# Four graph layers on one core: the order of all jobs of 32 graphs is computed in the kernel's source instead of being interleaved by hand-set start times

## The chip, the core and the metric

The kernel runs on one core of a Trainium2 chip. A core has a tensor engine (PE) that multiplies matrices, and whose weight loads are listed apart as PEld; a vector engine (DVE); an activation engine (ACT); GpSimd (POOL); and a sync engine (SP) that here only issues DMAs. PE reads SBUF and writes PSUM. Each engine works through its own queue in order, and engines wait for each other by semaphores. The metric is the device time of one execution in microseconds; less is better.

## The reference

Thirty-two graphs of 512 nodes with 256 features, each with a symmetric 512 x 512 adjacency, go through four layers. Each layer takes `h = max(layernorm(x), 0)` and adds its result to `x`. In layer 3 the transformer block has its own residuals and norms inside.

```python
def reference(x, adj, ...):                       # x (32, 512, 256) f32, adj (32, 512, 512) int32
    # layer 0: graph attention with 4 heads of 64
    Wh = (h @ W).reshape(B, N, 4, 64)
    e = leaky_relu(e_src[:, :, None] + e_dst[:, None], 0.2)      # e_src, e_dst: Wh times a_src, a_dst
    x = x + elu(softmax(where(adj > 0, e, -1e9), axis=2) @ Wh)
    # layer 1: one head, softmax over the other axis
    hw = h @ W;  e = leaky_relu(s1[:, :, None] + s2[:, None], 0.2)
    x = x + elu(softmax(where(adj > 0, e, -9e15), axis=1) @ hw)
    # layer 2: scores (h * a_0) h^T where adj == 1 (adj is 0 or 1 here)
    x = x + softmax(where(adj == 1, leaky_relu((h * a_0) @ h.T, 0.2), -9e15)) @ h
    # layer 3: transformer block, 8 heads of 32, feed-forward of 1024
    attn = softmax(where(allowed, q @ k.T / sqrt(32), -inf)) @ v
    t = layernorm(h + attn @ Wo.T + bo) * g1 + b1
    u = layernorm(t + relu(t @ W1.T + c1) @ W2.T + c2) * g2 + b2
    x = x + u
```

All data are 32-bit floats; the masks are bf16. One fp32 product of the source is two MATMUL instructions in the trace.

## The kernel before

Everything of interest is in `quick_path`. (`general_path` is a fallback behind a test at the end and does not run on these inputs.) A graph's 512 nodes are four tiles of 128 partitions, numbered by `i` or `j`; the features are two halves, numbered by `k`.

The Python loops unroll the whole program, so all 32 graphs lie in one straight stream of instructions. A graph passes three stages. Stage 0 loads `adj` and `x`, makes the masks (`masks`, L219 to L232: DVE makes a bf16 mask `m`, PE transposes it at L226, DVE copies it to `mT` and makes `m3` for layer 3) and does layer 0. Stage 1 does layers 1 and 2. Stage 2 does layer 3, the transformer block.

A norm (`norm_stats`, `normed`) is a chain: DVE statistics (L164, L165), POOL adds epsilon and takes the power -0.5 (L167, L168), DVE makes the shift (L170), ACT scales four tiles (L176). PE transposes follow (L185 for layers 0 to 2, L197 for layer 3).

Layer 0 computes `wh` (L257), sends per-row factors through DRAM to have them on all partitions (`spread`, L204 to L210), and for each of four heads lets DVE form four tiles `p` (L274) and PE sixteen products (L281). Layer 1 is alike with one head (L308, L320, L321, output products L333). Layer 2 has score products (L358), two exponentials on ACT, two DVE steps, and output products (L370).

Layer 3: products for q and k (L391) and v (L400); then eight steps of two groups of heads by four tiles, each with four score products (L419), two exponentials on ACT of 1024 columns (L430), a mask product on DVE of 2048 columns (L431), four products with v into `ps_ct` (L434) and four with ones into `ps_to` for the sums (L440). The sums of a group go out to DRAM, back in another layout, are inverted, and go out and back again, four DMAs on SP's queue (L448 to L456), and DVE multiplies them in (L459). Then the output projection (L467), an add (L469), a norm with PE transposes (L197) and ACT (L474), the two feed-forward products (L486 with ACT L487, and L493 with DVE L495), a last norm, two POOL operations (L498, L499) and the store (L500).

PSUM: `ps_a` has two tiles of one bank for layers 0 to 2, `ps_b` two tiles of two banks for layer 3, and `ps_ct` and `ps_to` have one bank each. In SBUF most activations of a stage have one buffer, so each stage holds one graph at a time. `x`, `mT` and `m3` have three.

What sets the order: each stage is a generator that yields a share of a period after each piece of work, and the main loop always advances the generator with the least due time. A graph's three stages start 0, 1.3 and 2.38 periods after its number:

```python
    STARTS = (0.0, 1.3, 2.38)
    live = [[b + at, stage(b)] for b in range(B) for at, stage in zip(STARTS, (stage0, stage1, stage2))]
    while live:
        now = min(live, key=lambda one: one[0])
```

That fixes the order in which instructions are written down. The tile framework's scheduler then takes this order as priority, reorders by its own estimates of durations, chooses buffers, and adds all semaphore waits. The scores of layer 3 have raised priority, with one added wait so that four heads go at a time. The final order in each engine's queue is fixed at compile time.

Of the kernel before, what the change touches and what calls it, by code (L numbers as in the profile page):

```python
# [1 line left out]

# [50 lines left out]

def quick_path(
# [21 lines left out]
    work = ctx.enter_context(tc.tile_pool(name="work", bufs=4))  # L76
    small = ctx.enter_context(tc.tile_pool(name="small", bufs=3))
    dram = ctx.enter_context(tc.tile_pool(name="dram", bufs=2, space=bass.MemoryType.DRAM))


    ps_a = ctx.enter_context(tc.tile_pool(name="ps_a", bufs=2, space=bass.MemoryType.PSUM))
    ps_b = ctx.enter_context(tc.tile_pool(name="ps_b", bufs=2, space=bass.MemoryType.PSUM))
    ps_c = ctx.enter_context(tc.tile_pool(name="ps_c", bufs=1, space=bass.MemoryType.PSUM))

    def load(b):
        adj_t = act.tile([P, NT, N], I32, tag="adj", name=f"adj_{b}")
        nc.sync.dma_start(adj_t, adj[b].rearrange("(t p) j -> p t j", p=P))
        x_t = act.tile([P, NT, D], F32, tag="x", name=f"x_{b}", bufs=3)
        nc.sync.dma_start(x_t, x[b].rearrange("(t p) d -> p t d", p=P))
        return adj_t, x_t  # L90

    loaded = {0: load(0)}
# [17 lines left out]
    src_r = rows_of(nc, work, a0_src, D, "src_r", "p", 6)  # L110
    dst_r = rows_of(nc, work, a0_dst, D, "dst_r", "p", 6)
    a1_r = rows_of(nc, work, a1, 2 * D, "a1_r", "p", 6)
# [13 lines left out]
    ff2b_r = rows_of(nc, work, ff2_b, D, "ff2b_r", "p", 6)  # L126
# [4 lines left out]
    for k in range(KD):  # L131
        for a_r, at, sign in ((src_r, D, -1.0), (dst_r, D + H0, 1.0)):
            wa = work.tile([P, N], F32, tag="y", name="wa")
            nc.vector.scalar_tensor_tensor(wa[:, :D], w0_t[:, k, :D], sign, a_r, OP.mult, OP.mult)
            nc.vector.tensor_reduce(
                w0_t[:, k, at : at + H0], wa[:, :D].rearrange("p (h f) -> p h f", h=H0), AX.X, OP.add
            )
        for at, sign in ((0, 1.0), (1, -1.0)):
            wa = work.tile([P, N], F32, tag="y", name="wa")
            nc.vector.scalar_tensor_tensor(  # L140
                wa[:, :D], w1_t[:, k, :D], sign, a1_r[:, at * D : (at + 1) * D], OP.mult, OP.mult
            )
            nc.vector.tensor_reduce(w1_t[:, k, D + at : D + at + 1], wa[:, :D], AX.X, OP.add)
# [3 lines left out]
    bv_w = work.tile([P, N], F32, tag="y", name="bv_w")  # L147
    ps = ps_a.tile([P, N], F32, tag="mm", name="ps_bv")
# [9 lines left out]

    def norm_stats(t):

        st = small.tile([P, NT, 6], F32, tag="st", name="st")
        mv = small.tile([P, NT, 2], F32, tag="mv", name="mv")
        for i in range(NT):
            nc.vector.bn_stats(st[:, i], t[:, i])  # L164
            nc.vector.bn_aggr(mv[:, i], st[:, i])  # L165
        rstd = small.tile([P, NT], F32, tag="rstd", name="rstd")
        nc.gpsimd.tensor_scalar_add(rstd, mv[:, :, 1], EPS)  # L167
        nc.gpsimd.tensor_tensor(rstd, rstd, nhalf, OP.pow)  # L168
        shift = small.tile([P, NT], F32, tag="shift", name="shift")
        nc.vector.scalar_tensor_tensor(shift, mv[:, :, 0], -1.0, rstd, OP.mult, OP.mult)  # L170
        return rstd, shift

    def normed(t, to, func):
        rstd, shift = norm_stats(t)
        for i in range(NT):
            nc.scalar.activation(to[:, i, :D], t[:, i], func, bias=shift[:, i : i + 1], scale=rstd[:, i : i + 1])  # L176
        return to

    def transposed_a(h, tag, name):

        hT = act.tile([P, KD, N], F32, tag=tag, name=name)
        for k in range(KD):
            ps = ps_a.tile([P, NT, P], F32, tag="mm", name="ps_t")
            for i in range(NT):
                nc.tensor.transpose(ps[:, i], h[:, i, ts(k, P)], ident)  # L185
            if k % 2:
                nc.scalar.copy(hT[:, k], ps.rearrange("p a b -> p (a b)"))
            else:
                nc.vector.tensor_copy(hT[:, k], ps.rearrange("p a b -> p (a b)"))
        return hT  # L190

    def transpose_b(t):

        ps = ps_b.tile([P, KD, N], F32, tag="mm", name="ps_t3")
        for k in range(KD):
            for i in range(NT):
                nc.tensor.transpose(ps[:, k, ts(i, P)], t[:, i, ts(k, P)], ident)  # L197
        return ps

    def spread(cols, n, name):  # L200


        ps = ps_a.tile([P, N], F32, tag="mm", name="ps_sp")
        nc.tensor.transpose(ps[: n * NT, :P], cols, ident)  # L204
        r = small.tile([H0 * NT, P], F32, tag="spread", name="spr")
        nc.vector.tensor_copy(r[: n * NT], ps[: n * NT, :P])
        d = dram.tile([n * NT, P], F32, tag=name + "d", name=name + "_d")
        nc.sync.dma_start(d, r[: n * NT])
        t = act.tile([P, n, N], F32, tag=name, name=name)
        nc.sync.dma_start(  # L210
            t, bass.AP(tensor=d.tensor, offset=d.offset, ap=[[0, P], [N, n], [1, N]])
        )
        return t

    def masks(b, adj_t):


        m = act.tile([P, NT, N], BF, tag="e_0", name=f"m_{b}")
        nc.vector.tensor_scalar_max(m, adj_t, 0)  # L219
        kinds = small.tile([P, 1], F32, tag="kinds", name="kinds")  # L220
        nc.scalar.activation(adj_t, adj_t, AF.Relu, bias=none, accum_out=kinds)
        mT = act.tile([P, NT, N], BF, tag="mT", name=f"mT_{b}", bufs=3)
        for j in range(NT):
            ps = ps_a.tile([P, NT, P], BF, tag="mm", name="ps_m")
            for i in range(NT):
                nc.tensor.transpose(ps[:, i], m[:, i, ts(j, P)], ident_b)  # L226
            nc.vector.tensor_copy(mT[:, j], ps.rearrange("p a b -> p (a b)"))
        m3 = act.tile([P, NT, N], BF, tag="m3", name=f"m3_{b}", bufs=3)
        nc.vector.tensor_max(m3, m, mT)
        for i in range(NT):  # L230
            nc.vector.tensor_max(m3[:, i, ts(i, P)], m3[:, i, ts(i, P)], ident_b)
        nc.vector.scalar_tensor_tensor(ok[:, 0:1], kinds, 0.0, ok[:, 0:1], OP.is_le, OP.mult)  # L232
        return mT, m3

    def within(t, n):

        nc.vector.scalar_tensor_tensor(ok[:, :n], t, RANGE, ok[:, :n], OP.is_le, OP.mult)
        nc.vector.scalar_tensor_tensor(ok[:, :n], t, 1.0 / RANGE, ok[:, :n], OP.is_ge, OP.mult)

    S0, S1, S2 = 1 / 24, 1 / 31, 1 / 74
# [4 lines left out]
    def layer0(b, x_t, mT):  # L247
        h = normed(x_t, act.tile([P, NT, D + 1], F32, tag="h_0", name=f"h0_{b}"), AF.Relu)
        hT = transposed_a(h, "hT_0", f"h0T_{b}")
        yield 1 * S0  # L250
        wh = act.tile([P, NT, H0, F0 + 1], F32, tag="wh_0", name=f"wh0_{b}")

        rt = small.tile([P, 3 * H0, NT], F32, tag="rt", name="rt0")
        for i in range(NT):
            ps = ps_a.tile([P, N], F32, tag="mm", name="ps_wh")
            for k in range(KD):
                nc.tensor.matmul(ps[:, : D + 2 * H0], hT[:, k, ts(i, P)], w0_t[:, k], start=k == 0, stop=k == KD - 1)  # L257
            nc.scalar.activation(wh[:, i, :, F0], ps[:, D + H0 : D + 2 * H0], AF.Exp, scale=SLOPE)
            nc.scalar.activation(rt[:, : 2 * H0, i], ps[:, D : D + 2 * H0], AF.Exp, scale=1.0 - SLOPE)  # L259
            nc.vector.tensor_mul(  # L260
                wh[:, i, :, :F0],
                ps[:, :D].rearrange("p (h f) -> p h f", h=H0),
                wh[:, i, :, F0 : F0 + 1].to_broadcast([P, H0, F0]),
            )
            yield 1 * S0
        rows = spread(rt[:, :H0].rearrange("p h t -> p (h t)"), H0, "rows0")
        yield 1 * S0
        o = act.tile([P, NT, D], F32, tag="h_0", name=f"o0_{b}")
        inv = rt[:, 2 * H0 :]
        for hd in range(H0):  # L270
            ps_t = []
            for j in range(NT):
                p = work.tile([P, N], F32, tag="p", name="p0", bufs=6)
                nc.vector.scalar_tensor_tensor(  # L274
                    p, rows[:, hd], rt[:, H0 + hd, j : j + 1], mT[:, j], OP.max, OP.mult
                )
                ps_t.append(p)
            ps = ps_a.tile([P, NT, F0 + 1], F32, tag="mm", name="ps_o")
            for i in range(NT):
                for j in range(NT):  # L280
                    nc.tensor.matmul(  # L281
                        ps[:, i], ps_t[j][:, ts(i, P)], wh[:, j, hd], start=j == 0, stop=j == NT - 1
                    )
                yield 1 * S0
            nc.vector.reciprocal(inv[:, hd], ps[:, :, F0])
            nc.vector.tensor_mul(
                o[:, :, ts(hd, F0)], ps[:, :, :F0], inv[:, hd].unsqueeze(2).to_broadcast([P, NT, F0])
            )

        e = act.tile([P, NT, D], F32, tag="e_0", name=f"e0_{b}")  # L290
        nc.scalar.activation(e, o, AF.Exp)
        nc.vector.scalar_tensor_tensor(e, e, 1.0, x_t, OP.min, OP.add)
        nc.vector.scalar_tensor_tensor(x_t, o, 0.0, e, OP.max, OP.add)
# [729 lines left out]
```

## Time and profile before

| | |
|---|---|
| median of 3 runs | 5052.46 us (5049.55 to 5053.34) |
| the profiled execution | 5052.43 us, its span 5050.7 us |
| instructions | 51957 |
| PE, ACT, POOL busy | 4361.3 us (86%), 1890.0 us (37%), 718.0 us (14%) |
| DVE busy | 2474.6 us (49%) |
| granted PE clock, mean | 0.915 of full speed |
| DMA | 144.58 MB, 29 GB/s on average |

The span runs from the first to the last instruction. Matmuls are pipelined and their ends are modelled, so a busy PE is not a PE at its peak; start-to-start distances say more. "Idle before <-releaser" is the time for which an engine stood still just before an instruction, with what released it. The granted clock is the share of full speed that the throttle allowed to PE.

### The profile page before, as it was taken

To read this page: it belongs to the slowest core of one execution; us is meant where nothing else is said; L and a number is where in the kernel's file an instruction comes from. 1 tells how busy PE (TensorE), PEld (TensorE's weight loads), DVE (VectorE), ACT (ScalarE), POOL (GpSimd) and SP (SyncE) were. 2 spreads that over 40 slices of the span, in tenths; PEclk is the share of its full clock that TensorE was granted. 3 is DMA by queue.
4 is the path that set the end of the run, shared out by engine and by line. 5 is a ranking of instruction groups with operands and counts; after the bars stand their busy time and mean duration, and the time that the engine had idled before them with its cause. 6 is when DMAs were issued, how large, how long until landed. Compare 5 with 4: busy or idle time off the path is not lost. (4 is left out here: it accounts for less than half of the span.)

```text
span 5050.7 us, 51957 instructions
## 1 busy us (share of the span) xinstructions
PE 4361.3 (86%) x20294; PEld 2595.8 (51%) x20294; DVE 2474.6 (49%) x5115; ACT 1890.0 (37%) x3297; POOL 718.0 (14%) x618
## 2 busy tenths in 40 slices
PE   5888889888899888898888898888988888988886
PEld 4555455555455554455554555544555545555543
DVE  4544554444554454544455544445544455544432
ACT  1333433333433333433334333334333343433332
POOL 0011111110111111111101111101111011111111
PEclk7889899989999999999899999999999989999998
DMA  2010010010000000100100100001000001000000
GB/s 98 26 34 26 26 34 24 28 34 25 27 26 30 30 26 26 35 24 28 34 26 26 34 24 28 30 22 34 25 27 34 26 26 34 24 28 22 5 13 14
DMA packets 95435, 144.58 MB, mean 29 GB/s; under 512 B 25168, under 2 KB 61520, under 8 KB 91088
## 3 DMA queue, kind: packets, MB, share of 16 engines
q1 hardware_dynamic: 88832, 136.21, 8.1%
q10 hardware_dynamic: 6352, 4.99, 0.3%
q8 instruction: 162, 2.65, 0.2%
q14 instruction: 89, 0.73, 0.1%
HBM read 122.96 MB, written 18.22 MB: 28 GB/s over the span
## 5 line engine op out<-in xcount | busy, mean ns | idle before, releaser
L431 DVE TENSOR_TENSOR p<-p,m 128x2048 f32<-128x2048 f32 x256 | 586.0, 2289 | 391.9 <-ACT p L430 384.5
L281 PEld LDWEIGHTS ps_o<-wh,p 128*128 128x128 f32 x4096 | 586.4, 212 | 240.3 <-issue 129.9
L430 ACT ACTIVATE p<-ps_s 128x1024 f32<-128x1024 f32 x512 | 501.6, 1019 | 455.6 <-PE ps_to L440 326.3
L281 PE MATMUL ps_o<-wh,p 128*128 128x65 f32 x4096 | 606.7, 294 | 67.3 <-DVE p L274 66.9
L486 PE MATMUL ps_f<-tT,ff_t 128*128 128x512 f32 x1024 | 582.2, 706 | 73.9 <-ACT f L487 46.6
L274 DVE SCALAR_TENSOR_TENSOR p<-rows,rt,mT 128x512 f32<-128x512 f32 x512 | 458.9, 918 | 98.6 <-PE ps_o L281 82.7
L493 PE MATMUL ps_f<-ff_t,f 128*128 128x256 f32 x2048 | 458.4, 380 | 2.0 <-DVE u L495 2.0
L176 ACT ACTIVATE h<-x,shift,rstd 128x256 f32<-128x256 f32 x512 | 268.9, 591 | 484.2 <-DVE shift L170 197.8
L167 POOL TENSOR_SCALAR rstd<-mv 128x4 f32<-128x4 f32 x192 | 55.6, 294 | 2701.1 <-DVE mv L165 2701.1
L440 PE MATMUL ps_to<-p,ones 128*32 128x512 f32 x2048 | 428.7, 606 | 0.0
L493 PEld LDWEIGHTS ps_f<-ff_t,f 128*128 128x128 f32 x2048 | 387.0, 190 | 73.5 <-issue 15.3
L486 PEld LDWEIGHTS ps_f<-tT,ff_t 128*128 128x128 f32 x1024 | 212.7, 222 | 345.2 <-issue 171.4
L419 PE MATMUL ps_s<-qk 32*128 32x512 f32 x2048 | 350.3, 643 | 30.3 <-ACT qk L392 24.9
L434 PE MATMUL ps_ct<-p,v 128*32 128x512 f32 x2048 | 346.5, 610 | 14.5 <-DVE p L431 14.5
L487 ACT ACTIVATE f<-ps_f,ff1b_c 128x512 f32<-128x512 f32 x256 | 175.3, 685 | 384.6 <-PE ps_f L486 384.6
L333 PE MATMUL ps_o<-wh,p 128*128 128x256 f32 x1024 | 269.1, 402 | 15.5 <-ACT wh L325 15.5
L358 PE MATMUL ps_e<-h2T,ha 128*128 128x512 f32 x512 | 254.0, 621 | 24.7 <-DVE ha L352 23.8
L333 PEld LDWEIGHTS ps_o<-wh,p 128*128 128x128 f32 x1024 | 187.2, 195 | 129.9 <-issue 60.0
L391 PE MATMUL ps_qk<-h3T,wqkv_t 128*128 128x512 f32 x512 | 245.8, 616 | 3.1 <-ACT h3T L381 3.1
L370 PE MATMUL ps_o<-h,p 128*128 128x257 f32 x1024 | 245.5, 382 | 1.5 <-DVE p L364 0.5
L370 PEld LDWEIGHTS ps_o<-h,p 128*128 128x128 f32 x1024 | 192.3, 191 | 53.1 <-issue 24.3
L260 DVE TENSOR_TENSOR wh<-ps_wh,wh 128x256 f32<-128x256 f32 x128 | 54.3, 424 | 317.1 <-ACT rt L259 317.0
(125 smaller groups left out, 5384.8 us busy)
## 6 DMA issues: line engine op xcount, KB each, us to landing
adj<-in_adj_dram SPq DMA_DIRECT2D x32, 1024.0 KB
rows<-rows_d SPq DMA_DIRECT2D x32, 1024.0 KB
x<-in_x_dram SPq DMA_DIRECT2D x32, 512.0 KB
rows<-rows_d SPq DMA_DIRECT2D x32, 512.0 KB
inv<-in_d SPq DMA_DIRECT2D x64, 256.0 KB
out_dram<-y SPq DMA_DIRECT2D x32, 512.0 KB
ff_t<-in_L_gnn_W_dram ACTq DMA_DIRECT2D x2, 1024.0 KB
to_d<-to SPq DMA_DIRECT2D x64, 8.0 KB
```

Source lines behind the costliest of these rows:

```text
L176: nc.scalar.activation(to[:, i, :D], t[:, i], func, bias=shift[:, i : i + 1], scale=rstd[:, i : i + 1])
L274: nc.vector.scalar_tensor_tensor(p, rows[:, hd], rt[:, H0 + hd, j : j + 1], mT[:, j], OP.max, OP.mult)
L281: nc.tensor.matmul(ps[:, i], ps_t[j][:, ts(i, P)], wh[:, j, hd], start=j == 0, stop=j == NT - 1)
L333: nc.tensor.matmul(ps[:, i], p[:, j, ts(2 * g + i, P)], wh[:, j, :D], start=j == 0, stop=j == NT - 1)
L370: nc.tensor.matmul(ps[:, : D + 1], p[:, j, ts(i, P)], h[:, j], start=j == 0, stop=j == NT - 1)
L419: mm = nc.tensor.matmul(ps[r // 2][:, r % 2], qk[at, KD + g, ts(j, P)], qk[at, g], start=True, stop=True)
L430: read = nc.scalar.activation(p[:, 2 * q : 2 * q + 2], ps[q], AF.Exp)
L431: nc.vector.tensor_mul(p, p, m3[:, j : j + 1].to_broadcast([P, HG, N]))
L434: nc.tensor.matmul(ps_ct[at], v[:, j, g * P + r * HD : g * P + (r + 1) * HD], p[:, r], start=j == 0, stop=j == NT - 1,)
L440: nc.tensor.matmul(ps_to[at], ones, p[:, r], start=j == 0, stop=j == NT - 1)
L486: nc.tensor.matmul(ps[:, q], ff1_t[:, k, ts(f, P)], tT[:, k], start=k == 0, stop=k == KD - 1)
L493: nc.tensor.matmul(ps[:, i], f1[f][:, f % 4, ts(i, P)], ff2_t[:, f], start=f == 0, stop=f == NF - 1)
```

## The change

A planner (`Plan`) takes the place of the generators. Instead of emitting an instruction, each step of each layer puts down a job: its engine, how long it occupies the engine (`takes`), when its result is there (`ends`), and what it reads and writes. Durations are constants written into the source: for DVE 0.155 us and 1.04 ns a column, for ACT 0.2 us and 0.81 ns, for a product of 512 columns 0.862 us (`FULL`), of 256 columns 0.432 us, for a step of four score heads 1.2 us, and so on. Buffers are `Kind`s with a number of slots; most are given out in the order in which the tiles were made (`in_turn`).

After the jobs of all 32 graphs are put down, graph by graph, `order` walks through time. At each moment each engine that is free takes, among the jobs whose inputs and slots are there, the one with the least key (graph number, then number of the job). `carry_out` then emits the jobs by planned start, with the planned slot, and ties each instruction to the one before it on its engine by an edge that only orders. Where a slot passes to a tile whose first engine is another one, a wait is added. PE's jobs are single products or short groups, and jobs of different graphs may alternate between them.

Beside this: within the layers the order of a few steps differs (the statistics of all four tiles come before their aggregates; the transposes of layer 3 go tile by tile; the tests `within` of layer 3 come after the add). The second feed-forward product goes into two tiles of `ps_a` where it went into one of `ps_b`. `ha` has the shape of `wh1`. The setup borrows other buffers. The counts and shapes of the products, DVE and ACT operations and DMAs stay as they are.

```diff
+class Plan:
+    HOP = 0.06
...
+    def put(self, engine, takes, ends, outs, ins, call, port=False):
+        j = Job()
+        j.key, j.engine, j.takes, j.ends, j.call, j.port = (self.key, len(self.jobs)), engine, takes, ends, call, port
...
+    def order(self):
+        engines = ("PE", "DVE", "ACT", "POOL", "SP")
...
+                while waiting[e]:
+                    key, one = heapq.heappop(waiting[e])
+                    take, then = slots(one)
+                    if take is not None:
+                        j = one
+                        break
...
+                j.start = max(now, port) if j.port else now
+                free[e] = j.start + j.takes
...
+                end = j.start + j.ends + self.HOP
...
+        return sorted(begun, key=lambda j: j.start)
+
+    def carry_out(self):
...
+        for j in self.order():
...
+                h.tile = kind.pool.tile(
+                    h.shape, h.dtype, tag=f"{kind.tag}_{h.slot}", name=h.name, bufs=1
+                )
...
+            for i in made:
+                if j.engine in last:
+                    self.tc.add_manual_dep(i, last[j.engine].name, edge, reason="as planned")
+                last[j.engine] = i
+            for kind, s in firsts:
+                if kind.last[s] is not None and kind.last[s][0] != j.engine:
+                    self.tc.add_manual_dep(made[0], kind.last[s][1].name, wait, reason="in turn")
...
+    def pool(self, method, *args, fixed=0.1, each=2.2e-3, **kw):
+        return self._do("POOL", self.nc.gpsimd, method, fixed, each, width(args), args, kw, True, 0.03)
...
+    K = {
+        tag: Kind(act, tag, slots)
+        for tag, slots in dict(
+            adj=1, x=3, mT=3, m3=3, h0=1, h0T=1, wh0=1, rows0=1, e0=1, p=6,
+            h1=1, h1T=1, wh1=1, rows1=1, p1=1, y=4, x2=2,
+            h3=1, hT3=1, qk=1, vt=1, p3=2, to=2, inv3=2, n=1,
+            kinds=2, rt0=2, rt1=2, inv2=2, part=4,
+        ).items()
+    }
...
+    K |= {"ps_ct": Kind(psum, "ps_ct", 1), "ps_to": Kind(psum, "ps_to", 1)}
+    K |= {"ps_a": Kind(psum, "ps_a", 2, False), "ps_b": Kind(psum, "ps_b", 2, False)}
...
-                p = work.tile([P, N], F32, tag="p", name="p0", bufs=6)
-                nc.vector.scalar_tensor_tensor(
-                    p, rows[:, hd], rt[:, H0 + hd, j : j + 1], mT[:, j], OP.max, OP.mult
+                p = new("p", "p0", [P, N])
+                plan.dve(
+                    "scalar_tensor_tensor", p, rows[:, hd], rt[:, H0 + hd, j : j + 1], mT[:, j], OP.max, OP.mult
                 )
...
+        for g in range(NT // 2):
+            ps = new("ps_a", "ps_f2", [P, 2, D])
...
-    STARTS = (0.0, 1.3, 2.38)
-    live = [[b + at, stage(b)] for b in range(B) for at, stage in zip(STARTS, (stage0, stage1, stage2))]
-    while live:
-        now = min(live, key=lambda one: one[0])
...
+    for b in range(B):
+        plan.key = b
+        adj_t = new("adj", f"adj_{b}", [P, NT, N], I32)
+        plan.dma(adj_t, adj[b].rearrange("(t p) j -> p t j", p=P), 9.0)
+        x_t = new("x", f"x_{b}", [P, NT, D])
+        plan.dma(x_t, x[b].rearrange("(t p) d -> p t d", p=P), 6.0)
         mT, m3 = masks(b, adj_t)
...
+        layer0(b, x_t, mT)
+        x_t = layer1(b, x_t, mT)
+        layer2(b, x_t, mT)
+        layer3(b, x_t, m3)
+    plan.carry_out()
```

## The prediction

> **What bounds the kernel now.** I read the page first, then the busy time by stretches, then the order of work on the tensor engine (PE), and last the rows of single instructions. The page says PE, and also that PE is not full: 86% busy, at a clock row that dips below 9 here and there.
>
> ```profile
> PE 4361.3 (86%) x20294; PEld 2595.8 (51%) x20294; DVE 2474.6 (49%) x5115; ACT 1890.0 (37%) x3297; POOL 718.0 (14%) x618
> ```
>
> The kernel does 32 equal graphs, so one period is what counts. Line L469 runs once per graph, and its first and last start give the period: (4995.1 - 288.0) / 31 = 151.84 us, with 288.0 before the first and 55.6 after the last.
>
> ```profile
> L469 DVE TENSOR_TENSOR t<-ps_wo,h x32: 1224/1225/1226, 288.0 to 4995.1; 128x1024 f32<-128x1024 f32 x32
> ```
>
> The busy time by stretches, for one period cut at four places (columns: stretch, length, busy us of PE, weight loads, DVE, ACT, POOL, granted clock, DMA share, GB/s):
>
> ```profile
> 2000.88:2032.66 31.78, 31.78 (x131) 24.00 (x129) 7.67 (x28) 6.98 (x18) 0.00 (x0) 1.00 0.10 34
> 2032.66:2047.78 15.12, 11.77 (x85) 10.46 (x84) 12.96 (x20) 7.23 (x17) 7.77 (x6) 1.00 0.01 2
> 2047.78:2115.61 67.83, 64.22 (x354) 30.63 (x354) 38.63 (x57) 31.64 (x48) 6.50 (x6) 1.00 0.10 28
> 2115.61:2150.60 34.99, 23.50 (x73) 12.30 (x73) 18.74 (x56) 13.11 (x20) 8.36 (x8) 0.80 0.12 39
> ```
>
> The feed-forward stretch is full. The last one is not: PE sits idle for 11.5 of 35 us and the clock falls to 0.80. Its order of work shows why:
>
> ```profile
> 2115.61 3.65 PE L358 MATMUL ps_e<-h2T,ha 128*128 128x512 f32 x8
> 2123.62 0.69 PE L226 MATMUL ps_m<-ident_b,m 128*128 128x128 bf16 x5 [4.36 <-DVE m L219]
> 2124.22 4.69 PE L467 MATMUL ps_wo<-wo_t,cT 128*128 128x256 f32 x14
> 2128.75 0.55 PE L226 MATMUL ps_m<-ident_b,m 128*128 128x128 bf16 x7
> 2130.56 0.38 PE L226 MATMUL ps_m<-ident_b,m 128*128 128x128 bf16 x4 [1.26 <-DVE mT L227]
> 2134.75 2.80 PE L197 MATMUL ps_t<-ident,n 128*128 128x128 f32 x8 [3.81 <-ACT n L176]
> ```
>
> PE's queue is in order. Its head is the next graph's mask transposes, which wait 4.36 us for DVE; then come transposes that wait 3.81 us for a norm. Meanwhile the middle graph's last p of layer 2 is written at about 2124.8, and its 7 us of output products (L370) run only from 2150.60. So this is a wait of order, not of data. It recurs in almost every graph:
>
> ```profile
> PE ps_m L226 <- DVE m L219: 132.2, 30, 5.6
> PE ps_t L197 <- ACT n L176: 122.3, 35, 5.4
> ```
>
> **The full-speed content of a period.** Matmul records overlap, so I take start to start where the clock is 1.00. For example 8 of L370 take 1.74 us and 4 of L486 take 1.72:
>
> ```profile
> 2000.88 1.91 PE L370 MATMUL ps_o<-h,p 128*128 128x257 f32 x8
> 2002.62 1.88 PE L486 MATMUL ps_f<-tT,ff_t 128*128 128x512 f32 x4
> 2004.34 1.05 PE L257 MATMUL ps_wh<-w_t,h0T 128*128 128x264 f32 x4
> ```
>
> Per graph, instructions times spacing: layer 3 (qk 16, 7.0; v 16, 3.9; scores 64, 8.6; ct 64, 7.0; to 64, 7.8; wo 16, 3.5; 16 transposes, 1.8; ff1 32, 13.8; ff2 64, 13.8) 67.2 us. The rest (L281 128, 15.5; L257 and L308 3.7 each; L333 7.3; L358 7.3; L370 7.0; 42 mask, norm and spread transposes, 4.3) 48.8 us. Together 116 us. Of 151.84 us, then, 36 are lost. In the period shown idle takes 18.4 of them (149.72 - 131.27), the slow clock some 6.5 (the last stretch holds about 17 us of content in its 23.50 busy), and the rest hides in the modelled busy time.
>
> **The change, part by part.** (1) The arithmetic stays: same matmuls, same DVE and ACT operations, same DMAs. Regrouping of tiles and the reordered statistics cost nothing, since the counts and shapes are the same. (2) The hand-set starts (0, 1.3, 2.38) and yields go, and with them the scheduler's own choice. A greedy plan takes their place: at each free engine the ready job of the oldest graph, then that of the next. The edges inside an engine are order only. The added cross-engine waits fire when a slot passes to a tile with another first engine; the slot was already awaited for its readers, so they add at most queue events (21 ns each in L274's rows) on perhaps ten tiles, 0.2 us a graph. Below nothing they cannot go; I take 0. (3) ff2 leaves the two large PSUM tiles for the two small ones. That frees ps_b for the next graph's layer 3 some 14 us earlier, and ties one of the small tiles for 6.9 us twice, while PE is full of ff2 anyway. I take 0, with ends of -3 (the next h3 transposes start earlier) and +2 (two 0.9 us ps_o jobs must drain first). (4) DMAs keep the SP queue, now in planned order. A transfer that waits for its source holds back those behind it, adj and x loads among them, but these are fetched a graph ahead. I take 0.
>
> What is left is how dense PE becomes. With the oldest graph first, layer 3 runs nearly alone at its own pace. Its chain: norm, transposes and copy 7 (statistics 1.0, POOL 0.23 + 1.04, shift 0.16, four ACT 2.08, transposes 0.3, copy 1.01, hand-overs); qk and v 10.9; attention 34 (eight loops of scores 1.07, two exps of 1.02 and hand-overs, 3.5 each, and 6 for the last product); the round trip of the sums 9.2 (2111.76 to the last issue at 2118.50 in this trace, and some 2.5 to land); cT 0.7, wo 3.5, t 1.2; norm to tT 7; ff1 13.8; ff2 with its add 14.5. That is 102 us with 67 of its own PE work, so 35 us of gaps. The younger graphs have 48.8 us of PE work to put there.
>
> How well are gaps filled? The attention stretch above packs about 57 us of content into 67.83 (84%), the poor one 17 into 35 (49%). Two younger chains of DVE, ACT and DMA steps feed the gaps, so I take three quarters: 26 us. The other 22.6 us come after layer 3, in the rest of the next graph's layers 1 and 2, at 80%: 28. So 102 + 28 = 130, and 1 us for filler jobs that cannot be interrupted: 131 us a graph. The best I can argue is 90% and 95% (102 + 18 = 120), the poorest half and 70% (102 + 45 = 147).
>
> The ends: graph 0 is held by its due times now (its layer 0 ends at about 79, h1T is copied at 101.3; its first product with the sums is at 261.7 and t only at 288.0). As the oldest it runs unhindered, so I take off 12, 7 and 24: t at 245, with 235 and 260 as bounds. The tail stays at 55, one graph alone.
>
> Sum: 245 + 31 x 131 + 55 = 4361, and the 1.7 us that the profiled execution (5052.43) has beside its span (5050.7): 4363. That execution stands 0.03 us from the median. I say 4360.
>
> **One rule against the plan.** DVE and POOL can block each other:
>
> ```profile
> 2041.87 0.72 DVE L274 SCALAR_TENSOR_TENSOR p<-rows,rt,mT 128x512 f32<-128x512 f32 x1
> 2042.73 2.36 POOL L498 TENSOR_TENSOR y<-y,g_r 128x1024 f32<-128x1024 f32 x1 [1.74 <-ACT y L176]
> 2042.84 5.57 DVE L274 SCALAR_TENSOR_TENSOR p<-rows,rt,mT 128x512 f32<-128x512 f32 x2
> ```
>
> Two L274 took 5.57 us beside POOL's large operations, against 0.74 each. Their mean is 918 ns against a median of 743, so 16 x 0.175 = 2.8 us a graph. The plan counts 0.687 for each and never sets its port flag for DVE. I keep 2.8 us of DVE time, inside the 80%. The Trainium skill (SBUF — State Buffer, Who interferes with whom) says more: any DVE instruction with two SBUF inputs and a GpSimd instruction that reads SBUF exclude each other for the whole instruction. By it 49 us of DVE work per graph are exposed to 14.4 us of POOL work, an estimate of 14.4 x 49 / 131 = 5.4 us a graph, and the total would be some 80 us higher than mine; no row of this trace shows the other DVE lines blocked.
>
> **The rivals.** *Starved middle graph (slower).* Oldest first gives the middle graph's layers 1 and 2 only leftovers. Unhindered they take about 60 us (two norms with transposes 12, products 3.7 + 7.3 + 7.3 + 7.0, spread 8, DVE and ACT steps 15). If all of it is left when layer 3 ends, the period is 102 + 60 = 162 and the total 245 + 31 x 162 + 57 = 5324. It decides from the point where more than 50 of the 60 us are left (102 + 50 = 152). Against it: 35 us of gaps, of which these layers need 28. Chance 0.12, slower cases short of full starvation included. *Drift.* The queues are in order, and fillers are placed the moment that the plan thinks them ready. Where DVE is late (L274, and up to 2.87 us once), PE's head waits, and the clock falls again as at 2124. Half of the gain is lost: period 143, total 245 + 31 x 143 + 57 = 4735. Chance 0.22. *Nearly packed.* Attention is planned at 3.4 us a step where rows give 2.93, so real PE runs ahead and the slack absorbs lateness; the clock stays at 1.00. Period 121, total 4053. Chance 0.16. *Nothing happens*, because the order in the queues comes out as before: 0.02; the explicit edges speak against it.
>
> **How the numbers follow.** My forecast has 0.48. The range takes in the nearly packed case with its lower bound (235 + 31 x 120 + 57 = 4012) and drift up to the poorest period (260 + 31 x 147 + 57 = 4874), and leaves out starvation and a little below. A run differs from no change from 0.2% on, about 10 us. Faster: 0.48 + 0.22 + 0.16, less 0.01 for the part of drift that goes too far, 0.85; same 0.02; slower 0.13.
>
> **What would show it.** Right: L469 every 131 us, L226's and L197's PE waits gone as heads of long idles, the clock at 0.96 or more, L370 of the next graph inside layer 3's norm. Wrong: idle PE before scores or before L308 to L370 just after an ff2 (starvation), PE waits on L274 or on DMA rows all over (drift), a clock still at 0.92.

## The result and the profile after

The change made the kernel slower: a median of 5321.59 us (5308.6 to 5335.09) against 5051.01 us (5037.19 to 5053.34) for the kernel before on the same chip, a ratio of 1.054 (95% interval 1.051 to 1.058). That is outside the predicted range. The total lies 2 us from the starved rival's 5324, and the period on it; the experiments show that this is an accident.

The profiled execution took 5324.7 us, its span 5322.9, with a mean granted clock of 0.888 (0.915 before). The first line is the busy time of each engine, the second the once-per-graph add that was L469. (In this kernel one helper line, L292, carries all DVE, ACT and POOL work, L310 the DMAs, and L320 and L322 PE's transposes and products; one reads by tiles.)

```profile
PE 4288.2 (81%) x20294; PEld 2583.6 (49%) x20294; DVE 2622.7 (49%) x5115; ACT 1896.6 (36%) x3297; POOL 751.4 (14%) x618
L292 DVE TENSOR_TENSOR t<-ps_wo,h x32: 1224/1225/1225, 237.8 to 5265.2; 128x1024 f32<-128x1024 f32 x32
```

PE is busy 73 us less than before in a span 272 us longer. The period is (5265.2 - 237.8) / 31 = 162.2 us where it was 151.84. The ends did shorten: the first add comes at 237.8 instead of 288.0. All of the loss lies in the steady state.

What PE waited for (total us, times, longest):

```profile
PE ps_ct L322 <- DVE p L292: 204.3, 140, 5.0
PE ps_wo L322 <- DVE cT L292: 149.0, 32, 10.7
PE ps_t L320 <- ACT n L292: 132.2, 32, 6.8
PE ps_f L322 <- ACT f L292: 100.5, 128, 0.8
```

The mask transposes, the largest wait before, are gone from the top. The norm's transposes kept theirs (122.3 before). Three waits are new or grown. Before, they stood at:

```profile
PE ps_ct L434 <- DVE p L431: 14.5, 34, 1.4
PE ps_wo L467 <- DVE cT L459: 26.7, 17, 6.9
PE ps_f L486 <- ACT f L487: 46.6, 29, 2.4
```

PE waited there for the masked `p` of layer 3, for `cT` and for ACT's `f`. Now the last comes 128 times, four in every graph, always about 0.8 us. A wait that recurs so exactly is built in.

DVE's own waits tell where its delay comes from; both of these stand in its list in every trip of the sums, two in each graph:

```profile
DVE cT L292 <- DMA inv<-in_d: 266.9, 64, 5.9
DVE part L292 <- DMA part<-to_d: 144.5, 64, 8.5
```

One such trip, from the order of work (start, duration, engine, work, and in brackets the idle time before it with its releaser):

```profile
2508.53 0.50 SPq L310 DMA_DIRECT2D to_d<-to  x1
2510.25 0.32 SPq L310 DMA_DIRECT2D part<-to_d  x1
2511.86 0.25 DVE L292 RECIPROCAL part<-part 128x16 f32<-128x16 f32 x1 [5.49 <-DMA part<-to_d]
2512.14 0.33 SPq L310 DMA_DIRECT2D in_d<-part  x1
2513.59 0.55 SPq L310 DMA_DIRECT2D inv<-in_d  x1
2518.69 0.69 DVE L292 TENSOR_TENSOR cT<-cT,inv 128x512 f32<-128x512 f32 x1 [4.19 <-DMA inv<-in_d]
2519.44 4.54 PE L322 MATMUL ps_wo<-wo_t,cT 128*128 128x256 f32 x12 [3.64 <-DVE cT L292]
```

From the first issue to the multiply are 10.16 us. DVE stands 5.49 and 4.19 us at the heads that the plan put there, and PE stands 3.64 us at its own. The granted clock pays too (stretches of 4 us, columns as in the prediction):

```profile
2516.00:2520.00 4.00, 0.56 (x3) 0.51 (x4) 1.31 (x4) 0.44 (x1) 0.00 (x0) 1.00 0.13 49
2520.00:2524.00 4.00, 4.00 (x12) 3.23 (x11) 2.37 (x8) 0.00 (x0) 0.10 (x1) 0.57 0.39 117
```

PE does 0.56 us of work in the first stretch, and in the next the clock is at 0.57.

**The plan against the chip.** The kernel's source ends its planning with a span of its own (`self.span`, no measurement): 4454.9 us for this kernel, with adds from 193.5 to 4404.3, a period of 135.8. Set job by job beside the trace, the chip is 44 us behind the plan at the first add and 861 us at the last, and the lag grows nearly in a straight line (by 21 to 30 us from graph to graph): 26.4 us a graph (162.2 - 135.8). So the plan is about as dense as forecast (135.8 against 131); the chip doesn't follow it. Two places in the source explain much of this.

*The DMAs.* In `order` a job that needs another job of its own engine becomes ready when that one's `takes` is over. For DVE or PE that is right. For SP `takes` is the issue, 0.1 us, not the landing. So the plan lets `part<-to_d` start 0.10 us after `to_d<-to`, and `inv<-in_d` 0.10 us after `in_d<-part`. In the trace the medians from issue to issue are 1.72 and 1.44 us. The plan also lets `inv` arrive 2.8 us after its issue, where the trace has 5.05 to the multiply. A trip planned at 5.4 to 6.1 us takes 10.3 (median of 64, 9.7 to 12.7).

*The halves of a two-bank tile.* Each tile of the first feed-forward takes four products, two for each bank, and ACT reads each bank by itself. The plan counts banks of 512 columns apart, so it has PE fill the second while ACT reads the first. The tile framework tracks the tile as a whole: its wait holds the fourth product until ACT has read the first half.

```profile
2536.93 3.70 PE L322 MATMUL ps_f<-tT,ff_t 128*128 128x512 f32 x8 [0.84 <-ACT f L292]
2541.41 3.70 PE L322 MATMUL ps_f<-tT,ff_t 128*128 128x512 f32 x8 [0.78 <-ACT f L292]
2545.89 2.41 PE L322 MATMUL ps_f<-tT,ff_t 128*128 128x512 f32 x5 [0.78 <-ACT f L292]
```

After every eight instructions, the four products of one tile, PE stands for 0.8 us. Against the plan a feed-forward loses 4.5 us here, and the products for q and k, built alike, 2.1 (medians of the 32 graphs).

### The profile page after: what moved, and what is told of

Same layout as the page of the kernel before. It is cut to its first block, busy times and chain, and to the rows that moved or that the text cites. A ratio compares the mean times of both kernels' runs of the same rounds, so it can differ in the third digit from the quotient of the medians.

```text
span 5322.9 us, 52024 instructions
## 1 busy us (share of the span) xinstructions
PE 4288.2 (81%) x20294; PEld 2583.6 (49%) x20294; DVE 2622.7 (49%) x5115; ACT 1896.6 (36%) x3297; POOL 751.4 (14%) x618
## 5 line engine op out<-in xcount | busy, mean ns | idle before, releaser
L322 PE MATMUL ps_o<-wh,p 128*128 128x65 f32 (+1 forms) x5120 | 826.2, 323 | 83.4 <-DVE o L292 63.7
L322 PEld LDWEIGHTS ps_o<-wh,p 128*128 128x128 f32 x5120 | 779.1, 217 | 178.2 <-issue 100.7
L292 DVE TENSOR_TENSOR p<-p,m 128x2048 f32<-128x2048 f32 x256 | 584.4, 2288 | 221.8 <-ACT p L292 221.7
L292 ACT ACTIVATE p<-ps_s 128x1024 f32<-128x1024 f32 x512 | 495.6, 1020 | 255.2 <-PE ps_s L322 255.2
L322 PE MATMUL ps_f<-tT,ff_t 128*128 128x512 f32 x1024 | 496.3, 623 | 101.4 <-ACT f L292 100.5
L292 POOL TENSOR_SCALAR rstd<-mv 128x4 f32<-128x4 f32 x192 | 74.9, 390 | 3249.0 <-DVE mv L292 2473.4
L322 PE MATMUL ps_ct<-p,v 128*32 128x512 f32 x2048 | 306.4, 673 | 205.0 <-DVE p L292 204.3
L322 PE MATMUL ps_f<-ff_t,f 128*128 128x256 f32 x2048 | 451.3, 380 | 9.1 <-DVE h2T L292 9.1
L292 DVE SCALAR_TENSOR_TENSOR p<-rows,rt,mT 128x512 f32<-128x512 f32 x512 | 403.1, 842 | 92.5 <-DMA rows<-rows_d 92.5
L292 ACT ACTIVATE h<-x,shift,rstd 128x256 f32<-128x256 f32 x512 | 270.1, 592 | 454.3 <-DVE shift L292 368.4
L322 PEld LDWEIGHTS ps_f<-ff_t,f 128*128 128x128 f32 x2048 | 387.7, 190 | 71.8 <-DVE h2T L292 12.8
L322 PEld LDWEIGHTS ps_f<-tT,ff_t 128*128 128x128 f32 x1024 | 191.2, 198 | 392.5 <-ACT f L292 207.0
L322 PE MATMUL ps_e<-h2T,ha 128*128 128x512 f32 x512 | 301.5, 731 | 62.0 <-DVE o L292 48.7
L292 ACT ACTIVATE y<-ps_e,nshift 128x512 f32<-128x512 f32 x256 | 161.2, 681 | 516.1 <-PE ps_e L322 516.1
L322 PE MATMUL ps_s<-qk 32*128 32x512 f32 x2048 | 300.7, 657 | 50.9 <-ACT p L292 49.8
L292 ACT ACTIVATE f<-ps_f,ff1b_c 128x512 f32<-128x512 f32 x256 | 175.9, 687 | 438.5 <-PE ps_f L322 436.8
L292 DVE TENSOR_TENSOR u<-ps_f,n 128x512 f32<-128x512 f32 x64 | 44.3, 692 | 569.2 <-PE ps_f L322 569.2
L322 PE MATMUL ps_wo<-wo_t,cT 128*128 128x256 f32 x512 | 190.2, 537 | 149.0 <-DVE cT L292 149.0
L320 PE MATMUL ps_t<-ident,h 128*128 128x128 f32 x1024 | 251.8, 361 | 69.4 <-ACT h L292 61.1
L322 PE MATMUL ps_to<-p,ones 128*32 128x512 f32 x2048 | 303.0, 666 | 0.0
L322 PE MATMUL ps_qk<-h3T,wqkv_t 128*128 128x512 f32 x512 | 253.7, 634 | 43.1 <-ACT qk L292 38.1
L320 PEld LDWEIGHTS ps_t<-ident,h 128*128 128x128 f32 x1024 | 145.9, 180 | 232.6 <-ACT h L292 130.2
```

What stands on the lines that cost most here:

```text
L292: return [getattr(unit, method)(*map(real, args), **{k: real(v) for k, v in kw.items()})]
L320: made.append(self.nc.tensor.transpose(*map(real, c)))
L322: made.append(self.nc.tensor.matmul(*map(real, c[:3]), start=c[3], stop=c[4]))
```

## The experiments

Theory A: the chip drifts behind because the plan's DMA times are too short. Theory B: it drifts because of the two-bank tiles. Rival C: the starved middle graph. The kernels are `after` with the edits shown. Each row has the plan's own span, the measured median, the ratio to the kernel before with its interval, and the granted clock.

| kernel | edits | own plan, us | chip, us | ratio (95%) | clock |
|---|---|---|---|---|---|
| after | | 4455 | 5321.59 | 1.054 (1.051 to 1.058) | 0.888 |
| e9_sums | two DMA edits | 4431 | 4958.17 | 0.984 (0.981 to 0.986) | 0.923 |
| e1_dma | three DMA edits | 4319 | 4802.77 | 0.952 (0.951 to 0.954) | 0.947 |
| e2_bank | tiles as a whole | 4446 | 5113.44 | 1.015 (1.013 to 1.017) | 0.896 |
| e3_both | e1 and e2 | 4328 | 4619.76 | 0.917 (0.914 to 0.920) | 0.950 |
| e4_noedge | no order edges | 4455 | 5255.9 | (one run) | 0.879 |
| e5_middle | middle graph first | 4447 | 5286.55 | 1.049 (1.046 to 1.051) | 0.888 |
| e6_ctpool | multiply on POOL | 4451 | 5263.2 | 1.045 (1.042 to 1.047) | 0.897 |
| e7_portdur | e3, times, port | 4474 | 4730.66 | 0.939 (0.937 to 0.941) | 0.927 |
| e8_keys | e7, other priority | 4293 | 4440.07 | 0.881 (0.878 to 0.884) | 0.951 |
| e10_noport | e8 without port | 4188 | 4469.17 | 0.886 (0.883 to 0.890) | 0.954 |
| e11_slack | e8, slack | 4307 | 4420.4 | 0.877 (0.875 to 0.879) | 0.954 |

The kernels ran in several sessions, each with the kernel before beside them; its median there lay between 5041.74 and 5051.01 us, so the differences between medians below are good to some 10 us.

### Longer DMA times in the plan: e1_dma

```diff
-                    k.ready = max(k.ready, free[e] if k.engine == e else end)
+                    k.ready = max(k.ready, free[e] if k.engine == e != "SP" else end)
...
-... [1, N]])), 3.5 + 1.2 * n
+... [1, N]])), 3.2 + 0.5 * n
...
-... [[N, HG], [0, HD], [1, N]])), 2.8
+... [[N, HG], [0, HD], [1, N]])), 5.0
```

No instruction is added or taken away. Only the order changes, by times as the trace shows them. (The second edit shortens the broadcast of `rows`. For layer 0 the plan had it at 8.4 us to DVE; the trace of after has 4.73, the median of the 18 times that DVE waited for it.)

> The plan alone is changed: a DMA that reads what the DMA before it wrote is ready when that one has landed (the plan took the moment of its issue, 0.1 us), inv lands after 5.0 us (was 2.8), and the rows after 3.2 + 0.5 n. The plan's own span goes from 4455 to 4319 us. Theory A (the plan believes in a round trip of the sums of 5.5 us that takes 10.8 on the chip, so DVE's queue stands at the multiply with inv and PE behind it): some 10 of the 27 us a graph by which the chip falls behind the plan go, and the kernel takes about 4319 + 870 - 320 - slow clock = 4750 us (4650 to 4900). Theory B (the two halves of a two-bank PSUM tile serialise, which the plan does not know): little of the lag goes, 5050 to 5200. Theory C (oldest graph first starves the younger graphs): no gain over the changed kernel beyond the plan's own, 5180 or more.

Measured 4802.77 us, 519 less than after, as A expected. DVE's waits:

```profile
DVE part L292 <- DMA part<-to_d: 81.9, 17, 5.8
DVE cT L292 <- DMA inv<-in_d: 17.8, 21, 5.9
```

The wait on `inv` fell from 266.9 to 17.8: the plan now puts other work ahead of the multiply. The clock rose from 0.888 to 0.947 with nothing done to it. The times for `rows` and the sums are told apart by e9_sums below.

### Two-bank tiles as the framework has them: e2_bank

```diff
-    i0, i1 = i0 // 512 * 512, i1 // 512 * 512 + 511
+    i0, i1 = i0 // 1024 * 1024, i1 // 1024 * 1024 + 1023
...
                 for k in range(KD):
                     plan.matmuls(FULL, (ps[:, q], ff1_t[:, k, cut(f, P)], tT[:, k], k == 0, k == KD - 1))
+            for q in (0, 1):
+                f = 2 * g + q
                 plan.act(
```

The four products of a tile come first, then ACT's two reads; the same in the products for q and k.

> Only the two-bank tiles of ff1 and q, k are treated otherwise: all four products first, then the two ACT reads, and the plan counts a two-bank tile as one. The plan's span stays (4446). Theory A: PE's waits of 0.8 to 1.0 us in ff1 and qk go (some 6 us a graph), the stand at inv stays: 5100 to 5200 us. Theory B: most of the lag goes, under 4900. Theory C: no change, 5300.

Measured 5113.44 us, 208 less than after. The lag had given 4.5 + 2.1 = 6.6 us a graph, 211 us in 32 graphs. The time lies in the range given under A. That the tiles make most of the lag, as B had it (under 4900), is refuted; they are a second and smaller cause beside A. What the runs show is a wait that the framework sets; whether the hardware would mind the two engines in the two banks was not tried.

### Both: e3_both

> Both edits together; the plan's span is 4328. If A and B are two separate parts of one cause, both gains add up: 4328 + 870 - 320 - 200 = 4680 and less where the clock stays up, 4450 to 4750 us, faster than the kernel before. Theory C: slower than the kernel before.

Measured 4619.76 us, 702 less than after; the two gains alone make 519 + 208 = 727. They add up nearly, so these are two separate losses. The feed-forward's 32 instructions now run in one piece, and the add's rows give a period of (4561.6 - 240.3) / 31 = 139.4 us:

```profile
2489.56 14.00 PE L322 MATMUL ps_f<-tT,ff_t 128*128 128x512 f32 x32
```

```profile
L292 DVE TENSOR_TENSOR t<-ps_wo,h x32: 1193/1224/1225, 240.3 to 4561.6; 128x1024 f32<-128x1024 f32 x32
```

This kernel's plan has 131.6. So of the 26.4 us by which a graph fell behind, 7.8 are left; the other 4.2 us of the gain are a shorter plan.

### The sums alone: e9_sums

The first and third edit of e1_dma, with `rows` left as it was.

> Of e1's edits only the two of the sums' round trip (ready when landed; inv after 5.0 us), not the shorter time of the rows. The plan's span is 4431, 24 us under the changed kernel's. Theory A: DVE's stand at inv goes, the lag falls by some 10 us a graph, and the time to 4900 to 5000 us, about 110 above e1. If e1's gain came from the rows, 5200 or more.

Measured 4958.17 us: the trip of the sums is worth 363 us, or 11.3 us a graph, and the times for `rows` the other 155 of e1_dma, of which 112 are a shorter plan (4431 to 4319). A time that is too long in the plan costs too. (The split is not sharp: the two DMAs of `rows` are on SP as well, so the first edit by itself lets the plan have `rows` later than before, and further from the trace.) The built-in wait is untouched here, as it should be:

```profile
PE ps_f L322 <- ACT f L292: 99.7, 128, 0.8
```

### The order edges taken out: e4_noedge

```diff
-                if j.engine in last:
-                    self.tc.add_manual_dep(i, last[j.engine].name, edge, reason="as planned")
```

The framework's scheduler may now reorder by its own estimates; the planned order is only its priority.

> The changed kernel without the edges that fix the order on each engine: planned starts are priorities only, and the framework's scheduler may reorder by its own estimates. Theory A and B (a fixed order with wrong durations makes heads of queues wait): the waits move elsewhere, and the time may fall to about the kernel before, 4900 to 5200 us. Theory C: as the changed kernel, 5300.

Measured 5255.9 us in its one run: 66 us better than after and above the 4900 to 5200 that A and B gave. So the edges alone don't make the loss. But the waits are others now:

```profile
PE ps_f L320 <- ACT f L290: 0.3, 1, 0.3
DVE cT L290 <- DMA inv<-in_d: 152.1, 64, 6.1
```

The first was 100.5 and the second 266.9 with the edges, and most of what they cost has come back elsewhere. How much of it is the planned order, which still holds as a priority, and how much the framework's own estimates, was not separated.

### The middle graph first: e5_middle

```diff
-        plan.key = b
+        plan.key = b + 0 - 1
...
+        plan.key = b + 0
         mT, m3 = masks(b, adj_t)
         layer0(b, x_t, mT)
+        plan.key = b + -1.5
         x_t = layer1(b, x_t, mT)
         layer2(b, x_t, mT)
+        plan.key = b + 0
         layer3(b, x_t, m3)
```

All of the plan's times stay wrong; layers 1 and 2 now go ahead of layer 3 of the graph before (and the loads of `adj` and `x` one graph ahead).

> The changed kernel with another priority and the wrong times of the plan kept: layers 1 and 2 of the middle graph come before layer 3 of the oldest. The plan's span stays (4447 against 4455). Theory C (oldest first starves the middle graph): the starving ends, and the time falls far below the changed kernel, to 4900 or less. Theories A and B (times that the plan has wrong): the same lag of 27 us a graph, 5200 to 5400 us.

Measured 5286.55 us, in the range given for A and B.

```profile
L292 DVE TENSOR_TENSOR t<-ps_wo,h x32: 1193/1224/1225, 280.1 to 5229.2; 128x1024 f32<-128x1024 f32 x32
```

The period is (5229.2 - 280.1) / 31 = 159.6 us, 2.6 less than after's and 25 above that of its own plan (134.5). By itself this run doesn't settle the rival, since its edit moves only a part of the leftovers: layer 2 of the next graph ends 13 us after the last product of layer 3, where it was 37 in after (means over the trace). Two other facts do. In after, the next graph's layer 1 begins its products 92 us before layer 3's last one, so it isn't all left over; and the priority with its leftovers is in the plan of after, at 135.8, and in e3_both, which keeps it and needs 139.4. What leads from 135.8 to 162.2 is not the priority.

### The multiply on POOL: e6_ctpool

```diff
-            plan.dve("tensor_mul", cT[:, g], cT[:, g], inv)
+            plan.pool("tensor_mul", cT[:, g], cT[:, g], inv)
```

This asks whether the harm of the late `inv` comes through DVE's queue, by letting another engine stand at it.

> The changed kernel with its wrong times, but the multiply of cT with inv is on POOL, not on DVE (1.23 us by the plan's own formula; plan's span 4451). Theory A says that DVE's queue stands at this multiply for some 267 us in all, and that this delays the products of attention: that wait is now POOL's, DVE's other one at the inversion of the sums (some 145 us) stays, and so does PE's own wait for cT: 5050 to 5200 us. If the stand of DVE's queue costs nothing because PE waits for cT anyway, 5300 to 5400.

Measured 5263.2 us, between the two expectations. DVE is free of the wait for `inv` (the one for `part` stays, 131.2 us), POOL bears it, and PE still stands at its own head:

```profile
POOL cT L292 <- DMA inv<-in_d: 1343.5, 52, 44.5
```

```profile
PE ps_t L320 <- ACT n L292: 183.8, 32, 6.2
PE ps_ct L322 <- DVE p L292: 106.2, 127, 2.5
PE ps_wo L322 <- POOL cT L292: 104.8, 16, 11.3
PE ps_wo L322 <- POOL h L292: 70.9, 16, 4.8
```

So taking DVE's stand at `inv` away is worth 58 us. What the rest of the 363 is was not tested. DVE's stand at `part` remains here, and PE's order, too, has `wo` where the plan believed `cT` ready: PE stands 175.7 us before those products, and 149.0 in after. (POOL's stand may delay its other work, the power step of the norms among it: the wait for `n` was 132.2 and is 183.8. So the 58 us may be too low.)

### Other priority and more exact times: e8_keys and e7_portdur

e7_portdur is e3_both with times from the traces, and with the planner told that DVE and POOL exclude each other:

```diff
     def dve(self, method, *args, each=1.04e-3, fixed=0.155, port=False, **kw):
+        both = {"scalar_tensor_tensor": (1, 3), "tensor_mul": (1, 2), "tensor_add": (1, 2), "tensor_max": (1, 2)}
+        if method in both:
+            port = not any(
+                isinstance(args[i], Part) and args[i].home.kind.tag.startswith("ps") for i in both[method]
+            )
...
-                    1.2,
+                    1.07,
...
-                    1.15,
+                    0.89,
...
-                plan.matmuls(1.05,
+                plan.matmuls(0.98,
```

(1.2, 1.15 and 1.05 were a step's four score products, the four with v and the four with ones. Some times get longer: L274's step has 0.743, and the `wh` products 0.47 and 0.455.) e8_keys has, beside this, keys that let the younger graphs go first, so that layer 3 of the oldest is no longer always ahead (the loads of `adj` and `x` go one more graph ahead):

```diff
+        plan.key = b + -2.5
         mT, m3 = masks(b, adj_t)
         layer0(b, x_t, mT)
+        plan.key = b + -0.5
         x_t = layer1(b, x_t, mT)
         layer2(b, x_t, mT)
+        plan.key = b + 0.0
         layer3(b, x_t, m3)
```

> The repaired plan (both edits of e3) that also lets a DVE step with two SBUF inputs and a POOL step exclude each other, has the durations of the chip for the attention products and two-input steps, and another priority: layer 0 of the youngest first, then layer 3 of the oldest, then layers 1 and 2. The plan's span is 4293 (with oldest first 4474). If the chip falls behind the plan by 4 to 8 us a graph, 4430 to 4560 us, faster than e3. If counting the port costs more than it saves, as e3 or slower, 4620 and up.

> e8 with the priority of the changed kernel (oldest graph first); the plan's span is 4474 against e8's 4293 and e3's 4328. If the priority makes e8's gain over e3, this kernel is at 4474 and 140 of lag, 4580 to 4680 us. If counting port and durations makes it, it is near e8, 4450 to 4530.

e8_keys measured 4440.07 us, e7_portdur 4730.66. With the planner's times mended, the priority is worth 291 us, and the oldest-first rule of the change is the poorer one; already the two plans differ by 181 (4474 and 4293). e7 missed both of its expectations, since it is even slower than e3_both (4619.76). Its plan is looser by itself, 4474 against 4328; whether by the counted port or by the longer times was not separated. So whom a plan lets go first does matter here, but only where the plan is followed. In e5_middle, with wrong times, a priority moved the time by 35 us.

### Without the port in the plan: e10_noport

e8_keys without the `both` edit.

> e8 without the port in the plan: DVE steps with two SBUF inputs and POOL steps may again be planned side by side; the plan's span is 4188 against 4293. If DVE and POOL block each other on the chip as e8's plan has it, the chip falls back by the difference and more, 4400 to 4520 us. If the blocking costs nothing where PE is the bound, 4330 to 4400, faster than e8.

The plan is 105 us shorter (4188), and the chip is no faster: 4469.17 us (4444.34 to 4488.98) against 4440.07 (4426.35 to 4449.72). What the plan leaves out comes back on the chip.

### Some slack: e11_slack

```diff
-    HOP = 0.06
+    HOP = 0.12
...
-... max(open_, key=lambda s: kind.free[s])
+... min(open_, key=lambda s: kind.free[s])
```

Every hand-over gets 0.06 us more in the plan, and of the free slots the one longest free is taken.

> e8 with a hand-over of 0.12 us in the plan (was 0.06) and the slot that has been free longest taken first (was: the one freed last); the plan's span is 4307 against 4293. If the lag that e8 has left (about 140 us) comes from hand-overs without slack, 4380 to 4430 us. If it comes from the slow clock and the port, 4430 to 4470.

4420.4 us, the lowest median of all: a ratio of 0.877 to the kernel before (0.875 to 0.879), with a period of (4363.2 - 267.5) / 31 = 132.1.

```profile
L292 DVE TENSOR_TENSOR t<-ps_wo,h x32: 1217/1224/1226, 267.5 to 4363.2; 128x1024 f32<-128x1024 f32 x32
```

The edit adds 14 us to the plan and takes 20 from the chip, which is no more than what the runs of one kernel differ by. The time lies in the range given for hand-overs without slack, but so small a step, made of two edits, doesn't show that they were the rest of the lag.

## Why the prediction was wrong

**The ends were right.** First add at 245, measured 237.8; tail 55, measured 5322.9 - 5265.2 = 57.7. For the first add there is luck in it: the plan has 193.5, and 44 us of lag made up the difference.

**The density of the order was right, and not the question.** I worked out 131 us a graph from a layer-3 chain and gaps filled to three quarters. The plan says 135.8 and the repaired e3_both's plan 131.6. (That e11_slack does 132.1 on the chip is no test of the sum, since it has another priority.) The sum described what a plan of this kind can do. On the chip both of its parts came out longer: from the first q and k product of a graph to the last feed-forward product 117.2 us, where the chain without its first norm has 95, and from there to the next graph's first q and k product 44.9, where I had 28 and a norm of 7 (means over the trace of after). The sum did not ask whether the chip can follow this one: whether each time in the source, and each rule by which a job becomes ready, agrees with the trace.

**The step that failed first: "(4) DMAs keep the SP queue … I take 0".** The queue's order is as I said. But in the new `order` a DMA's duration decides where *other* engines' queues put their work, and `order`'s line for jobs of one engine was in the code to be read. The plan's trip of the sums is about 5.5 us, and I used 9.2 for the chain without setting the two beside each other. Mending the trip gave 11.3 us a graph (e9_sums), and the times for `rows` 4.9 more (155 / 32), of which 3.5 are a shorter plan.

**The term that was mis-sized: "some 2.5 to land".** The trip that I read doesn't show it, because DVE was busy with other work until its multiply at 2123.48. But in 14 of the 64 trips in the trace of before DVE stood waiting for `inv`, 4.59 to 5.99 us after its issue (median 5.0). The last one:

```profile
4983.53 0.60 SPq L456 DMA_DIRECT2D inv<-in_d  x1
4988.55 0.69 DVE L459 TENSOR_TENSOR cT<-cT,inv 128x512 f32<-128x512 f32 x1 [5.95 <-DMA inv<-in_d]
```

5.02 us are twice what I took, and against them the source's 2.8 would have stood out.

**The second step that failed: the regrouping of tiles "cost nothing", and (3) "I take 0" for PSUM.** Counts and shapes are the same, and so much was right. But the order within a tile became the plan's, and the plan believes that a tile's halves are separate. Before, the wait for `f` came 29 times, now 128 times; 208 us (e2_bank).

**The rivals.** Drift was the right mechanism: planned as forecast, late by a steady amount, PE waiting in order and a lower clock (0.57 after the gap shown). Its price was too low, 143 for 162.2, because I took lateness to come from L274 and to cost half of the gain. It cost more than all of it. The starved rival's 162 and 5324 agree with the result to a few us, by a mechanism that isn't the cause: layers 1 and 2 last some 37 us beyond layer 3's end, not 60, and e3_both has the same priority at 139.4 us. A total that agrees shows no cause. The forecast had counted on idle PE before scores or L308 to L370 as the sign of starvation, and the list of waits is led by `ct`, `wo`, `n` and `f`.

**The clock.** I asked for 0.96 if right and 0.92 if wrong; it was 0.888. With the same products it is higher where PE idles less: PE is idle for 1035 us of the span in after, 771 in e1_dma (0.947) and 482 in e11_slack (0.954). This isn't strict, since e7_portdur has 0.927 with 684, and what else bears on it was not tested.

**The rule on DVE and POOL.** I took 2.8 us a graph from L274's rows; by the Trainium skill (SBUF — State Buffer, Who interferes with whom) the estimate was 5.4. In after, the time above each line's median, summed over five DVE lines (L274's 50.8, the norm's shift 40.3, layer 2's mask product 32.4, layer 1's `e` 25.9, `y` 17.5), is 167 us, or 5.2 a graph. All 96 instances that took over 100 ns more than their line's median ran beside a POOL instruction. The rule was nearer than my row, though with after's own period the same estimate would be 14.4 x 49 / 162.2 = 4.4. In e8_keys it is 6.4 a graph (204 us in three lines), with the plan counting it.

**What stays open.** After e11_slack's plan of 129.8 us a graph the chip needs 132.1, and PE's content at full speed was 116. How the distance divides between the plan's own gaps, the clock and blocked DVE work was not separated. Nor is it shown why e7_portdur's plan is looser than e3_both's.

## What to carry to other kernels

An order that is fixed in advance is worth what its times are worth: before pricing how dense it is, set every duration and every readiness rule of the planner beside the trace, those of DMAs and of dependences inside one queue first, since an engine in order turns one short guess into idle time for all behind it. When such a kernel is slow, compare planned and measured starts job by job; a lag that grows by the same amount in each period is built into the order; the waits that recur in each period point to the edge that is wrong, and mending that edge alone tests it. A rival whose total agrees with the result still has to be tested by taking its mechanism away.

## What the runs showed of the hardware

What a small trip through DRAM took in after (medians of 64): 8 KB written and read back 1.72 us from issue to issue and 1.68 more to its reader, and the 256 KB broadcast 5.05 us from its issue to its reader.

More DVE lines than L274 are lengthened beside POOL. Layer 2's two steps (minimum/median/maximum in ns), first before, then after:

```profile
L363 DVE TENSOR_TENSOR y<-y,y x128: 681/686/694, 153.1 to 4865.6; 128x512 f32<-128x512 f32 x128
L364 DVE TENSOR_TENSOR p<-y,mT x128: 647/685/693, 153.8 to 4866.3; 128x512 f32<-128x512 f32 x128
```

```profile
L292 DVE TENSOR_TENSOR y<-y,y x128: 679/692/1805, 136.9 to 5177.4; 128x512 f32<-128x512 f32 x128
L292 DVE TENSOR_TENSOR p<-y,mT x128: 691/692/2722, 137.6 to 5178.2; 128x512 f32<-128x512 f32 x128
```

The medians agree, the longest went from 693 to 2722 ns. In before none of these 256 instructions ran beside a POOL instruction; in after all 32 that took over 100 ns more than the median did. So a line without long instances may only never have met POOL, and an order that is made anew brings other instructions together. One more line of before had been blocked, once, beside POOL's product of `n` and `g_r`, which the prediction overlooked:

```profile
L170 DVE SCALAR_TENSOR_TENSOR shift<-mv,rstd x192: 161/164/2297, 19.9 to 5038.9; 128x4 f32<-128x4 f32 x192
```
